# Attention row terms by a transpose and a DRAM round trip in place of TensorE transposes, with the batch's steps moved around it

## The chip, the cores and the metric

One core of one Trainium2 chip runs the whole kernel; the other cores are idle. The metric is the device time of a run in microseconds (us), and a kernel's time is the median of its runs. TensorE is called PE below, VectorE DVE, ScalarE ACT, GpSimd POOL, and the queue from which most DMAs are issued SP.

## What is computed

The input x has 64 batches of 256 rows of 256 numbers, and an adjacency matrix of 256 x 256 is shared by all batches. Each batch passes through four blocks, each with a layer norm in front and a residual sum behind. The first attention, which the change is about, has four heads:

```python
q = (norm(x) @ W).reshape(B, N, H=4, 64)
e_src, e_dst = q @ a[:64], q @ a[64:]                 # two numbers per row and head
e = e_src[:, :, None, :] + e_dst[:, None, :, :]
e = where(e >= 0, e, 0.2 * e)
attn = softmax(where(adj > 0, e, -9e15), axis=2)
x = x + elu(einsum('bijh,bjhd->bihd', attn, q))
x = x + norm(x) @ weight.T + bias
# a second attention of the same kind with one head (slope 0.01, relu)
# a mixture of 8 experts, the best 2 for each row: y = gelu(t @ w1[e]) @ w2[e]
```

The kernel never forms the sum e. The exponential of a leaky rectifier of a sum is the larger of two products, so it takes exponentials of per-row terms, and one vector instruction per half of a head gives `max(term of row i, term of row j) * mask`. For that it needs the term of row i along the free dimension, the same in all 128 partitions, while the term of row j lies in partition j already. This row of terms, spread over all partitions, is what the change makes in another way.

## The kernel before

**Steps and ranks.** The program is written in order of *steps*; three steps make a *period*, in which one batch enters and two pairs of expert blocks are worked on (phases 0, 1 and 2). Every batch and every pair is a generator. A `yield` of a positive number ends its work in this step, and the number is its rank in the next one: within a step the generators run in order of rank. A negative number leaves it in the same step, to be taken up again at that rank. Engines get their instructions in the order so made and work through them in order; an engine that waits for a semaphore holds all that is behind it. The main loop at L1138 starts batches, pairs and the scattering of results.

**A batch** (`batch_layers`, L537). In phase 2 DVE turns the batch's input into a transposed tile (L542). In phase 0 the statistics of the first norm are taken (L547; POOL raises them to the power -1/2 at L383, two norms at a time). In phase 1 `projected` (L549, matmuls at L436) makes the four heads and their terms, ACT takes the exponentials (L444), and DVE scales the heads (`scaled`, L452). In the next phase 2 and phase 0 `scores` does two heads each: PE transposes the term column, broadcast to 128 x 128, against the identity (L506), which leaves the row of terms in all partitions of a PSUM bank, and DVE forms max and mask from it (L513). In the next phase 1 `attended` multiplies (L527). Later steps do the residual, the second norm, the dense layer (L584), the second attention (`projected1`, L471; `scores1`, L495), the expert input (L635, L640), and the router (L665). ACT copies every PE transpose from PSUM to SBUF at L426.

**The pairs** (`expert_pair`, L783). A pair is 256 gathered rows of one expert. It starts in phase 1 and requests its rows there (`xr`, four DMAs at L799, and `xt`, L810), one step later its weights (`we`, L825, seven buffers). Two steps after the start DVE turns the rows (`sT`, L116), two steps on PE does the first product (L857), then the second (L872). In the last steps, when no batch is left to enter, a pair starts in every step.

**The DMA queues.** All of a period's loads and stores of these kinds are issued by SP in one order: `xr` and `xt` of the two pairs, `xblk` (the blocks that L542 turns), the two `we`, `xin` (the rows for the norm and the residual), and `out_dram<-base` (L651), which waits for ACT's L640. As the program is built, a DMA issued by SP or ACT takes one of eight semaphores in turn, in one sequence over both queues, and its issue waits until the DMA that had this semaphore eight places earlier has landed. ACT issues six DMAs in all, at the start.

Of the kernel before, what the change touches and what calls it, by code (L numbers as in the profile page):

```python
# [9 lines left out]
F32 = mybir.dt.float32  # L10
# [5 lines left out]
P = 128  # L16
# [11 lines left out]
def kernel(  # L28
# [17 lines left out]
    nc = tc.nc  # L46
    B, N, D = x.shape
    E = router.shape[0]
    H = 4
# [44 lines left out]
    def load_batch(b):  # L94
        t = io.tile([P, NT, D], F32, tag="xin", name=f"xin_{b}", bufs=6)
        nc.sync.dma_start(
            out=t, in_=x_rows[b * N : (b + 1) * N, :].rearrange("(t p) d -> p t d", p=P)
        )
        return t
# [10 lines left out]
        return t  # L110

    S = 32

    def turned(dst, blocks):

# [371 lines left out]
    def scores1(ex, me):  # L487
        pd = bank("pd", [N])
        for t in range(NT):
            nc.tensor.transpose(  # L490
                pd[:, t * P : (t + 1) * P], ex[:, t, 1:2].to_broadcast([P, P]), ident
            )
        z = work.tile([P, NT, N], F32, tag="z", name="z", bufs=6)
# [6 lines left out]
    def scores(q, heads, hs, mask, probs):  # L500

        d = D // heads
        pd = bank("pd", [len(hs), N])
        for i, h in enumerate(hs):
            for t in range(NT):
                nc.tensor.transpose(  # L506
                    pd[:, i, t * P : (t + 1) * P],
                    q[:, t, h, d + 1 : d + 2].to_broadcast([P, P]), ident,
                )
        for i, h in enumerate(hs):  # L510
            z = work.tile([P, NT, N], F32, tag="z", name="z", bufs=6)
            for j in range(NT):
                nc.vector.scalar_tensor_tensor(  # L513
                    z[:, j, :], pd[:, i, :], q[:, j, h, d + 2 : d + 3], mask[:, j, :],
                    op0=ALU.max, op1=ALU.mult,
                )
            probs.append(z)

    def attended(q, heads, probs):

        d = D // heads
        pvs = []
        for t in range(NT):
            pv = bank("pv", [heads, d + 1])
            for h, z in enumerate(probs):
                for j in range(NT):
                    nc.tensor.matmul(  # L527
                        pv[:, h, :], z[:, j, t * P : (t + 1) * P], q[:, j, h, : d + 1],
                        start=(j == 0), stop=(j == NT - 1),
                    )  # L530
# [6 lines left out]
    def batch_layers(b, c0, xng, lg):  # L537

        xb = xblk.pop(b)
        if b + BLOCKS_AHEAD < B:  # L540
            xblk[b + BLOCKS_AHEAD] = load_blocks(b + BLOCKS_AHEAD)
        xT = turned(work.tile([P, KT, N], F32, tag="xT", name="xT", bufs=4), xb)  # L542
        yield 40
        x0 = xin.pop(b)
        if b + AHEAD < B:
            xin[b + AHEAD] = load_batch(b + AHEAD)
        _, rstd = norm_stats(x0)  # L547
        yield 20
        q, pqs = projected(xT, wx0, H, rstd)  # L549
        yield -28  # L550
        scaled(q, pqs, H, rstd)
        yield 10
        probs = []
        scores(q, H, range(0, 2), masks[0], probs)
        yield 10
        scores(q, H, range(2, 4), masks[0], probs)
        yield 50
        pvs, rinv = attended(q, H, probs)
        hp = work.tile([P, NT, D], F32, tag="hp", name="hp", bufs=1)

        early = b < EARLY
# [12 lines left out]
        x1b = work.tile([P, NT, D], F32, tag="x1b", name="x1b", bufs=1)  # L574
        eng = nc.gpsimd if early else nc.vector
        eng.tensor_add(x1b, x1, bias_f[:, None, :].to_broadcast([P, NT, D]))
        yield 30
        _, rstd = norm_stats(x1)
        xT = transposed(x1)
        yield 70  # L580
        pf = bank("pf", [NT, D])
# [12 lines left out]
            )  # L594
        yield 7
        rstd = norm_squares(x2, sums)
        yield -60
        xT = transposed(x2)
        yield 20
        q, ex, me = projected1(xT, rstd, b)  # L600
        yield 25
        z = scores1(ex, me)
        yield 40
        pvs, rinv = attended(q[:, :, None, :], 1, [z])
        yield 5
        rel = work.tile([P, NT, D], F32, tag="rel", name="rel", bufs=1)
        for t, pv in enumerate(pvs):
# [9 lines left out]
            )  # L617
        yield 6
        rstd = norm_squares(x2, sums)
        yield 45  # L620

        by = small.tile([P, 2, NT], F32, tag="by", name="by")
        nc.vector.scalar_tensor_tensor(  # L623
# [159 lines left out]
    def expert_pair(j, n, ids, ef, regs, needs):  # L783

        i = j % GROUP
        upto = min(j + GROUP, n)
        if i == 0:
            _, regs["e"] = nc.values_load_multi_w_load_instructions(
                ids[0:1, 0, j:upto], engines=[mybir.EngineType.SP], min_val=0, max_val=E - 1,
                skip_runtime_bounds_check_because=WHY,  # L790
            )
            _, regs["t"] = nc.values_load_multi_w_load_instructions(
                ids[0:1, 1, j:upto], engines=[mybir.EngineType.SP], min_val=0, max_val=E * CAP,
                skip_runtime_bounds_check_because=WHY,
            )
        e_sp, t_sp = regs["e"][i], regs["t"][i]
        xr = io.tile([P, PAIR // S, KT * S], F32, tag="xr", name="xr", bufs=XBUFS)
        loads = [
            nc.sync.dma_start(  # L799
                out=xr[g * S : (g + 1) * S],  # L800
                in_=xs_d.rearrange("(t c q) f -> t q c f", c=PAIR // S, q=S)[
                    bass.ds(t_sp, 1), :, :, g * KT * S : (g + 1) * KT * S
                ].rearrange("t q c f -> (t q) c f"),
            )
            for g in range(P // S)
        ]

        xt = small.tile([P, 2, ROW - D], F32, tag="xt", name="xt", bufs=14)
        loads.append(
            nc.sync.dma_start(  # L810
                out=xt,
                in_=xs_d.rearrange("(t k p) c -> t p k c", p=P, k=2)[
                    bass.ds(t_sp, 1), :, :, D:
                ].rearrange("t p k c -> (t p) k c"),
            )
        )
        for load in loads:
            tc.add_to_no_dep_group("rows", load.ins)
# [138 lines left out]
    def begin(job, rank):  # L957
        active.append([rank, len(order), job])
        order.append(job)
# [255 lines left out]
```

## Time and profile before

| | us |
|---|---|
| median of 3 runs (lowest, highest) | 1562.9 (1556.77, 1562.9) |
| the profiled execution's own time | 1554.1 |
| its span, first to last instruction | 1552.2 |
| PE busy over the span | 1476.8 (95%) |
| DVE busy | 1210.8 (78%) |
| ACT busy | 1015.3 (65%) |
| POOL busy | 881.0 (57%) |
| q1, SP's DMA queue: share of 16 DMA engines | 36.5% |
| q0, POOL's DMA queue: share of 16 DMA engines | 23.2% |

The page is of one profiled execution. Busy time is per engine; instructions that only wait or issue a DMA are not counted. A group line gives source line, engine, operation, tiles and shapes, count, then busy time in all, mean ns of one, and the idle time just before the group with what ended it. PE's instructions are pipelined, so that "busy" and the mean of one overlap with the next; the distance between the starts of two groups is what a group costs. A line of the chain or of the waits names who waited for whom. The wait rows give total us, times and the longest. The first pairs are requested at 198 us, the last first-layer transposes run at 1279 us, and the rest of the span is expert work.

### The profile page before, as it was taken

Reading aid. Unit: us, or ns where it says so; the run is one execution under the profiler, and the core shown is the slowest. Engines: PE = TensorE matmul, PEld = TensorE weight load, DVE = VectorE, ACT = ScalarE, POOL = GpSimd, SP = SyncE. Lnnn points to the kernel's source line nnn. Section 1 sums busy time; section 2 is a strip of 40 time slices with the busy share of each in tenths; the row PEclk is TensorE's granted clock in tenths of the full one; section 3 lists DMA queues with packets and bytes.
Section 4 is the critical chain, followed back from the end, with each engine's and each line's share of the span. In section 5 each row is a group of like instructions: output and inputs, shape, how many; then the busy total and the mean of one; then the engine's idle time right before and its main releaser. Section 6 shows DMA issues by size and latency. Waiting matters only on the chain. (4 is left out here: it accounts for less than half of the span.)

```text
span 1552.2 us, 30789 instructions
## 1 busy us (share of the span) xinstructions
PE 1476.8 (95%) x8570; PEld 1308.1 (84%) x8570; DVE 1210.8 (78%) x4313; ACT 1015.3 (65%) x2387; POOL 881.0 (57%) x867
## 2 busy tenths in 40 slices
PE   6999999999999999999999999999999998879997
PEld 5888888888888888888888888888888987668885
DVE  6888888888888888888878888888788778555543
ACT  1566666767677676776767777766678888654332
POOL 2222645466657575656667575755765566644444
PEclk9999999999999999999999999999999999889999
DMA  5812233665657666566656666566586575688853
GB/s 153 224 51 69 90 101 87 158 132 131 148 127 168 134 130 141 140 137 142 138 129 153 133 159 138 127 136 143 127 178 144 111 145 115 132 200 173 156 100 51
DMA packets 361514, 207.61 MB, mean 134 GB/s; under 512 B 261496, under 2 KB 331648, under 8 KB 361344
## 3 DMA queue, kind: packets, MB, share of 16 engines
q1 hardware_dynamic: 311488, 138.31, 36.5%
q0 software_dynamic: 48864, 66.33, 23.2%
q8 instruction: 71, 1.16, 0.3%
q10 hardware_dynamic: 992, 0.99, 0.2%
q14 instruction: 99, 0.81, 0.2%
HBM read 117.43 MB, written 88.09 MB: 132 GB/s over the span
## 5 line engine op out<-in xcount | busy, mean ns | idle before, releaser
L893 POOL DMA_INDIRECT out_dram<-y,xt x258 | 410.2, 1590 | 179.8 <-issue 75.8
L527 PE MATMUL pv<-q,z 128*128 128x65 f32 (+1 forms) x2560 | 364.1, 297 | 0.0
L527 PEld LDWEIGHTS pv<-q,z 128*128 128x128 f32 x2560 | 328.0, 192 | 11.5
L872 PE MATMUL py<-w2s,hT 128*128 (+1 forms) x1224 | 284.3, 383 | 6.8 <-ACT hT L863 6.2
L965 POOL DMA_INDIRECT xs<-xng,pos x244 | 251.5, 1031 | 65.8 <-issue 58.6
L872 PEld LDWEIGHTS py<-w2s,hT 128*128 128x128 f32 x1224 | 229.7, 192 | 39.7 <-ACT hT L863 9.0
L426 ACT COPY xT<-pt 128x512 f32<-128x512 f32 x192 | 112.8, 588 | 210.8 <-PE pt L420 148.5
L857 PE MATMUL ph<-sT,we 128*128 128x256 f32 x1032 | 241.1, 384 | 0.2 <-DVE sT L116 0.2
L857 PEld LDWEIGHTS ph<-sT,we 128*128 128x128 f32 x1032 | 194.2, 193 | 25.6 <-DVE sT L116 0.7
L513 DVE SCALAR_TENSOR_TENSOR z<-pd,q,mask 128x256 f32<-128x256 f32 x512 | 210.9, 473 | 0.0
L863 ACT ACTIVATE hT<-ph,we 128x256 f32<-128x256 f32 x306 | 124.2, 471 | 63.2 <-PE ph L857 41.1
L471 PE MATMUL pq<-wx,xT 128*128 128x259 f32 x512 | 133.6, 405 | 25.3 <-ACT xT L426 19.0
L850 ACT ACTIVATE y<-y,w 128x256 f32<-128x256 f32 x258 | 112.1, 499 | 69.2 <-DVE y L882 55.5
L382 POOL TENSOR_SCALAR rstd<-mv 128x4 f32<-128x4 f32 (+1 forms) x66 | 15.7, 238 | 221.7 <-DVE by L623 203.9
L471 PEld LDWEIGHTS pq<-wx,xT 128*128 128x128 f32 x512 | 94.6, 195 | 53.0 <-ACT xT L426 28.4
L882 DVE TENSOR_TENSOR y<-py,b2s 128x512 f32<-128x512 f32 x129 | 86.3, 687 | 63.4 <-PE py L872 49.9
L401 ACT ACTIVATE off<-x,sums 128x256 f32<-128x256 f32 x256 | 129.3, 505 | 8.5 <-DVE x L591 1.1
L436 PE MATMUL pq<-wx,xT 128*128 128x268 f32 x512 | 130.2, 398 | 3.3 <-DVE xT L116 2.7
L584 PE MATMUL pf<-wfT,xT 128*128 128x256 f32 x512 | 121.3, 380 | 0.0
L635 ACT ACTIVATE xng<-x,by,rstd 128x256 f32<-128x256 f32 x128 | 70.1, 597 | 74.9 <-DVE by L623 74.8
L436 PEld LDWEIGHTS pq<-wx,xT 128*128 128x128 f32 x512 | 97.1, 194 | 21.3 <-issue 3.3
L534 DVE RECIPROCAL rinv<-pv 128x4 f32<-128x4 f32 (+1 forms) x256 | 39.0, 166 | 84.9 <-PE pv L527 65.6
(164 smaller groups left out, 2537.5 us busy)
## 6 DMA issues: line engine op xcount, KB each, us to landing
we<-wpack SPq DMA_DIRECT2D x145, 288.0 KB
xr<-xs SPq DMA_DIRECT2D x516, 64.0 KB
xblk<-in_x_dram SPq DMA_DIRECT2D x256, 64.0 KB
xin<-in_x_dram SPq DMA_DIRECT2D x64, 256.0 KB
out_dram<-base SPq DMA_DIRECT2D x61, 256.0 KB
out_dram<-y,xt POOLq DMA_INDIRECT x258
xs<-xng,pos POOLq DMA_INDIRECT x244
xs<-fill SPq DMA_DIRECT2D x9, 260.0 KB
```

Source lines behind the costliest of these rows:

```text
L401: nc.scalar.activation(off, src[:, t, :], AF.Square, bias=sums[:, t : t + 1], scale=-float(D), accum_out=sq[:, at + t : at + t + 1],)
L426: nc.scalar.copy(dst, pt)
L436: nc.tensor.matmul(pq.rearrange("p h c -> p (h c)"), xT[:, k, t * P : (t + 1) * P], wx[:, k, :], start=(k == 0), stop=(k == KT - 1),)
L471: nc.tensor.matmul(pq, xT[:, k, t * P : (t + 1) * P], wx1[:, k, :], start=(k == 0), stop=(k == KT - 1),)
L513: nc.vector.scalar_tensor_tensor(z[:, j, :], pd[:, i, :], q[:, j, h, d + 2 : d + 3], mask[:, j, :], op0=ALU.max, op1=ALU.mult,)
L527: nc.tensor.matmul(pv[:, h, :], z[:, j, t * P : (t + 1) * P], q[:, j, h, : d + 1], start=(j == 0), stop=(j == NT - 1),)
L584: nc.tensor.matmul(pf[:, t, :], xT[:, k, t * P : (t + 1) * P], wfT[:, k, :], start=(k == 0), stop=(k == KT - 1),)
L857: nc.tensor.matmul(ph[:, f, :], we[:, k * D + f * P : k * D + (f + 1) * P], xT[:, k, :], start=(k == 0), stop=(k == KT - 1),)
L863: nc.scalar.activation(hT[:, f, :], ph[:, f, :], AF.Gelu, bias=we[:, C_B1 + f : C_B1 + f + 1])
L872: nc.tensor.matmul(py[:, t, :], hT[:, f, t * P : (t + 1) * P], w2s[:, e, f * D : (f + 1) * D].rearrange("p e c -> p (e c)"), start=(f == 0 ...
L893: d = nc.gpsimd.indirect_dma_start(out=out_rows, out_offset=bass.IndirectOffsetOnAxis(ap=xt[:, t, 0:1].bitcast(I32), axis=0), in_=y[:, t, ...
L965: d = nc.gpsimd.indirect_dma_start(out=xs_d[: E * CAP * PAIR, :], out_offset=bass.IndirectOffsetOnAxis(ap=at, axis=0), in_=xe, in_offset=None,
```

## The change

- **Terms.** The eight PE transposes per batch (L506) are gone. After `scaled`, DVE transposes in 32 x 32 blocks four columns of each head of q (128 x 32 numbers) into `ut`; ACT's queue stores the rows that hold the terms to a small DRAM tile (4 KB, one per batch); a second DMA of ACT's queue reads these 4 KB back into all 128 partitions (512 KB written), straight into one half of a new tile `z4`. `scores` then reads both its tensors from SBUF and writes over that half at its end. The second attention's z has a tile of its own with one buffer.
- **Order.** The first norm is taken when the batch begins, now in phase 0, one period before its projection. The projection moves from phase 1 to phase 0, directly behind `projected1` of an earlier batch; `scaled`, the transpose and the store follow in the same step at rank 24, the spreading load at rank 52. `scores` and `attended` stay in the phases where they were, which is two and more steps later.
- **Others.** The PE transposes for L471 move ahead of the second attention's product in their step (rank 60 to 36). The `by` terms for L635 move from rank 45 to 8. The transposes for the dense layer go to rank 30, the statistics ahead of them to 21.
- **Pairs.** `we` is requested in the same step as `xr` and `xt`, one step earlier than before.

In the program as built, ACT's order in phase 0 becomes: exponentials of the second and first attention, the store (waits for DVE's `ut`), the copy for the dense layer, L635 and L640's work, the spreading load (waits for the store), the scaling of y. The 128 new DMAs take their turn in the sequence of eight semaphores. SP's order in a period becomes `xr`, `xt`, `we` of one pair, the same of the other, `xblk`, `xin`, `out_dram<-base`. In most periods the two new DMAs stand in the sequence so that two of the four `xblk` loads, or one and `xin`, wait for them. In every fourth period, for batches 22, 26 and so on to 54, it is the first `xr` of the second pair that waits for the store, and that pair's `we` that waits for the spreading load.

```diff
+    def send_terms(q, b):
+        ut = small.tile([P, S], F32, tag="ut", name="ut", bufs=1)
+        nc.vector.transpose(
+            ut.rearrange("p (t h w) -> p t h w", t=NT, h=H), q[:, :, :, HD - 1 : HD + 3]
+        )
+        ud = tc.dram_tile([S, S], F32, name=f"terms_{b}")
+        ud = ud.rearrange("c r -> (c r)").rearrange("(c p) -> c p", p=P)
+        return ut, ud
+
+    def spread_terms(ud):
+        z = work.tile([P, NT, NT, H, P], F32, tag="z4", name="z4", bufs=2)
+        nc.scalar.dma_start(
+            out=z[:, NT - 1].rearrange("p t h i -> p (t h i)"),
+            in_=rows_to_all(ud, S * S),
+        )
         return z
...
-        pd = bank("pd", [len(hs), N])
-        for i, h in enumerate(hs):
-            for t in range(NT):
-                nc.tensor.transpose(
-                    pd[:, i, t * P : (t + 1) * P],
-                    q[:, t, h, d + 1 : d + 2].to_broadcast([P, P]), ident,
-                )
...
+        for h in hs:
             for j in range(NT):
                 nc.vector.scalar_tensor_tensor(
-                    z[:, j, :], pd[:, i, :], q[:, j, h, d + 2 : d + 3], mask[:, j, :],
+                    z[:, j, :, h, :], z[:, NT - 1, :, h, :], q[:, j, h, HD + 2 : HD + 3],
+                    masks[0][:, j, :].rearrange("p (t i) -> p t i", t=NT),
                     op0=ALU.max, op1=ALU.mult,
                 )
...
+        if b:
+            x0, rstd = first_norm()
+            yield 99
+            yield 25
...
-        yield 40
-        x0 = xin.pop(b)
-        if b + AHEAD < B:
-            xin[b + AHEAD] = load_batch(b + AHEAD)
-        _, rstd = norm_stats(x0)
-        yield 20
+        if not b:
+            x0, rstd = first_norm()
+        yield 22
         q, pqs = projected(xT, wx0, H, rstd)
-        yield -28
+        yield -24
         scaled(q, pqs, H, rstd)
+        ut, ud = send_terms(q, b)
+        nc.scalar.dma_start(
+            out=ud.rearrange("c (g r) -> g c r", g=G),
+            in_=ut[2 : P : S // (NT * H), :],
+        )
+        yield -52
+        z = spread_terms(ud)
+        yield 99
         yield 10
...
-        yield 30
+        yield 21
         _, rstd = norm_stats(x1)
+        yield -30
         xT = transposed(x1)
...
-        yield -60
+        yield -36
         xT = transposed(x2)
...
-        yield 45
+        yield 8
...
-        yield 90
         we = io.tile([P, WROW], F32, tag="we", name="we", bufs=WBUFS)
         nc.sync.dma_start(
             out=we, in_=wpack[bass.ds(e_sp, 1), :, :].rearrange("e p c -> (e p) c")
         )
+        yield 90
...
-            if phase == 2 and more:
+            if more and (phase == 0 or step == 2):
...
-                    begin(nxt, 25)
+                    begin(nxt, 40 if phase == 0 else 25)
```

More of the change, by code (lines that the diff above doesn't have):

```diff
@@ L112 @@
     S = 32
+    G = P // S
     def turned(dst, blocks):
@@ L492, in scores1 @@
             )
-        z = work.tile([P, NT, N], F32, tag="z", name="z", bufs=6)
+        z = work.tile([P, NT, N], F32, tag="z1", name="z1", bufs=1)
         for j in range(NT):
@@ L497, in scores1, with scores, attended @@
             )
-        return z
-    def scores(q, heads, hs, mask, probs):
-        d = D // heads
-        pd = bank("pd", [len(hs), N])
-        for i, h in enumerate(hs):
-            for t in range(NT):
-                nc.tensor.transpose(
-                    pd[:, i, t * P : (t + 1) * P],
-                    q[:, t, h, d + 1 : d + 2].to_broadcast([P, P]), ident,
-                )
-        for i, h in enumerate(hs):
-            z = work.tile([P, NT, N], F32, tag="z", name="z", bufs=6)
+        return [z[:, j, :] for j in range(NT)]
+    def send_terms(q, b):
[12 more added lines that the diff above has]
+        )
+        return z
+    def scores(q, z, hs):
+        for h in hs:
             for j in range(NT):
                 nc.vector.scalar_tensor_tensor(
-                    z[:, j, :], pd[:, i, :], q[:, j, h, d + 2 : d + 3], mask[:, j, :],
+                    z[:, j, :, h, :], z[:, NT - 1, :, h, :], q[:, j, h, HD + 2 : HD + 3],
+                    masks[0][:, j, :].rearrange("p (t i) -> p t i", t=NT),
                     op0=ALU.max, op1=ALU.mult,
                 )
-            probs.append(z)
-    def attended(q, heads, probs):
+    def attended(q, heads, z):
         d = D // heads
@@ L524, in attended @@
             pv = bank("pv", [heads, d + 1])
-            for h, z in enumerate(probs):
+            for h in range(heads):
                 for j in range(NT):
                     nc.tensor.matmul(
-                        pv[:, h, :], z[:, j, t * P : (t + 1) * P], q[:, j, h, : d + 1],
+                        pv[:, h, :], z(j, h, t), q[:, j, h, : d + 1],
                         start=(j == 0), stop=(j == NT - 1),
@@ L537, in batch_layers, with first_norm @@
     def batch_layers(b, c0, xng, lg):
+        def first_norm():
+            x0 = xin.pop(b)
+            if b + AHEAD < B:
+                xin[b + AHEAD] = load_batch(b + AHEAD)
+            return x0, norm_stats(x0)[1]
+        if b:
+            x0, rstd = first_norm()
+            yield 99
+            yield 25
         xb = xblk.pop(b)
@@ L542, in batch_layers @@
         xT = turned(work.tile([P, KT, N], F32, tag="xT", name="xT", bufs=4), xb)
-        yield 40
-        x0 = xin.pop(b)
-        if b + AHEAD < B:
-            xin[b + AHEAD] = load_batch(b + AHEAD)
-        _, rstd = norm_stats(x0)
-        yield 20
+        if not b:
+            x0, rstd = first_norm()
+        yield 22
         q, pqs = projected(xT, wx0, H, rstd)
-        yield -28
+        yield -24
         scaled(q, pqs, H, rstd)
+        ut, ud = send_terms(q, b)
[6 more added lines that the diff above has]
+        yield 99
         yield 10
-        probs = []
-        scores(q, H, range(0, 2), masks[0], probs)
+        scores(q, z, range(0, 2))
         yield 10
-        scores(q, H, range(2, 4), masks[0], probs)
+        scores(q, z, range(2, 4))
         yield 50
-        pvs, rinv = attended(q, H, probs)
+        pvs, rinv = attended(q, H, lambda j, h, t: z[:, j, t, h, :])
         hp = work.tile([P, NT, D], F32, tag="hp", name="hp", bufs=1)
@@ L603, in batch_layers @@
         yield 40
-        pvs, rinv = attended(q[:, :, None, :], 1, [z])
+        pvs, rinv = attended(
+            q[:, :, None, :], 1, lambda j, h, t: z[j][:, t * P : (t + 1) * P]
+        )
         yield 5
```

## The prediction

> **What bounds the kernel now.** I read the busy time by stretches first, then PE's timeline over one period, the groups by shape, the waits, and SP's timeline. In the stretches, columns are length, busy time of PE, weight loads, DVE, ACT, POOL, then PE's granted clock and DMA share:
>
> ```profile
> core 0: us, PE busy (x) PEld busy (x) DVE busy (x) ACT busy (x) POOL busy (x), PEclk, DMA share, GB/s
> 350.00:1050.00 700.00, 692.36 (x4151) 619.94 (x4152) 575.52 (x1985) 498.86 (x1183) 443.27 (x423) 1.00 0.64 140
> ```
>
> While batches and pairs run together PE is busy 99%, DVE 82%, ACT 71%. PE is the bound; DVE is near enough to become it. One period on PE's timeline (start, length):
>
> ```profile
> 649.85 2.02 PE L471 MATMUL pq<-wx,xT 128*128 128x259 f32 x8 [0.24 <-issue]
> ...
> 663.39 0.60 PE L506 MATMUL pd<-ident,q 128*128 128x128 f32 x4
> 663.82 3.62 PE L857 MATMUL ph<-sT,we 128*128 128x256 f32 x16
> ...
> 668.09 1.98 PE L527 MATMUL pv<-q,z 128*128 128x257 f32 x8
> 669.91 0.60 PE L420 MATMUL pt<-ident,x 128*128 128x128 f32 x4
> 670.35 0.60 PE L506 MATMUL pd<-ident,q 128*128 128x128 f32 x4
> 671.18 1.15 PE L471 MATMUL pq<-wx,xT 128*128 128x259 f32 x4 [0.24 <-issue]
> ```
>
> From L471 to L471 it takes 21.33 us. Four transposes cost 663.82 - 663.39 = 0.43 us, though each shows 0.27. L471 comes 0.83 us after the last four, so 0.4 us is idle: only those four (0.43) cover ACT's copy of L420's result. The waits name it (us, times, longest), and show who holds SP:
>
> ```profile
> PEld pq L471 <- ACT xT L426: 28.4, 36, 3.4
> ...
> SPq L651 <- ACT base L640: 420.8, 47, 15.4
> ```
>
> The groups show the work that goes or changes side (busy us, mean ns):
>
> ```profile
> L506 PE MATMUL pd<-ident,q 128*128 128x128 f32 x512 | 77.1, 274 | 3.4 <-ACT q L444 3.4
> L513 DVE SCALAR_TENSOR_TENSOR z<-pd,q,mask 128x256 f32<-128x256 f32 x512 | 210.9, 473 | 0.0
> L614 DVE SCALAR_TENSOR_TENSOR x<-x,rel 128x256 f32<-128x256 f32 x128 | 48.7, 417 | 0.0
> ```
>
> And SP's timeline, with DVE's use of the rows it loads:
>
> ```profile
> 679.77 0.40 SPq L651 DMA_DIRECT2D out_dram<-base  x1
> 682.52 1.55 SPq L799 DMA_DIRECT2D xr<-xs  x4
> ...
> 685.22 1.86 SPq L799 DMA_DIRECT2D xr<-xs  x4
> ...
> 699.88 0.40 SPq L651 DMA_DIRECT2D out_dram<-base  x1
> ```
>
> ```profile
> 700.67 1.30 DVE L116 STREAM_TRANSPOSE sT<-xr 128x512 f32<-128x512 f32 x2
> ```
>
> SP issues a period's loads in 12 us and waits 9 for L640; rows requested by 687 are used at 700.7. An issue takes 0.4 to 0.5 us.
>
> **The Trainium skill.** "Trainium Kernel Development and Optimization", Performance Expectations, warns that matmul busy time misleads because matmuls are pipelined; the trace agrees, 0.43 for four against 0.27 each, so I price starts, not L506's 77.1 us. "Perfetto Trace Analysis", Optimizing Scalar/DVE Operations, puts DVE's access overhead at about 60 ns on SBUF and 125 on PSUM; L614 against L513, both 256 wide, differ by 56 ns. "DMA: Bandwidth & Descriptors", Anatomy of one DMA (told of POOL's path), gives some 2 us fixed, mostly the write receipt; L651's stores, from issue to the last landing in the trace, take 2.0 us in the median, so I use that. "SBUF — State Buffer", Who interferes with whom, says that a DVE instruction with two SBUF inputs contends with a POOL instruction that reads SBUF; POOL's L411 runs from 189 to 744 ns here, DVE's L614 only from 411 to 471, so POOL pays.
>
> **The change part by part.** My clock is 0 at L471's start, with the rows' own distances.
>
> *Transposes gone.* 2 x 0.43 = 0.87 us per batch on the bound, x 64 = 56 us.
>
> *L420 ahead of L527.* L527's 1.82 us (669.91 - 668.09) now covers the copy: 0.4 more, x 64 = 25 at most. A period would be 21.33 - 1.26 = 20.07. The order on PE is L471 0 to 1.85, L436 to 3.66, L420 to 4.1, L872 to 7.55, L490 and L527 to 11.3, L420 (expert input), L584 to 13.53, L857 to 17.0, L665, L420 to 18.2, L527 to 20.07.
>
> *DVE.* Eight L513 at 417 instead of 473 ns save 0.45 us; `ut` is not in the trace. It is L116's operation at a sixteenth of its 700 ns width: 0.1 to 0.7, I take 0.2. DVE stays at 17.5 us of 20.1, 87%. Behind `ut` are the norm of x, y and sT, with 0.5 to 1 us of cover before PE's L857 asks.
>
> *ACT.* Exponentials end at 4.7; `scaled` (2 x 0.4) and `ut` at 5.9. The store waits for that, about 1.2 us in which all of ACT stands: the dense copy, L635, L640, L850. It issues in 0.45; copy and L635, L640 take until 9.1, L850 until 10.8. PE asks for L635 at 11.3 and for the next copy at 11.8: 1 us of cover. When routing lengthens DVE's queue by 1 to 2.5 us (its small operations, one batch in four most), this cover is gone and L471 waits again; I charge 0.2 us a batch, 10 in all. Bounds: 0, and 0.6 a batch, 30.
>
> *Round trip.* Store issued 6.0, landed 8.1; spreading load issued about 8.3, under L640. Its 128 reads of 4 KB are four times `bias_f`'s and twice `xin`'s 256 KB, which lands in 4.0 us (median in the trace). I take 4.7, landed at 13; bounds 3.5 and 9. DVE asks at 16.6, so 3.6 us cover it; if it landed at 19, 2.4 us of DVE wait meet 2.6 us of DVE slack. Its packets, at the 0.16 us of the trace's 4,160-byte packets, take 128 x 0.16 / 16 = 1.3 us of all DMA engines a period: DMA share 0.64 to 0.70.
>
> *Norm earlier.* ACT's L444 waited 22.7 us in all for POOL's L383, mostly in the first batches; DVE and POOL do the same work. I count nothing; its xin load moves no further ahead than its buffers. `by` at rank 8 lets L635 start without its 75 us of waits: cover for the ACT sum above, no gain by itself.
>
> *SP.* In most periods `xblk` now waits for both new DMAs, so SP resumes at 13 and `out_dram<-base` goes at about 15 instead of 9; the second pair's rows are requested by 20.5 and land by 23.5, wanted at 29. No cost. `we` earlier removes no PE wait, since none on it is listed; its two issues push the second pair's rows back 0.5 us, covered. In nine batches (22 to 54 by fours) the second pair's rows wait for the store: requested 8.1 to 10.2, landed at 12.2 (2.0 to 2.8 us as now), while DVE wants them at 9.1. It stands 3 us, L591 comes 1.7 late, and L471 with it; its `we` is requested at 13, lands at 16.3, for an L857 at 15.3. I take 1.7 us a batch, 15 in all; bounds 5 and 40.
>
> *First 14 batches, without pairs.* Of a period of 14.4 us (L471 at 110.0 and 124.4) DVE is busy 85%, and routing makes some 16.3. DVE takes PE's place as the bound, and `by` waits for POOL behind L576. I give them 0.5 instead of 1.26: 10 us less. *Last batches*: new waits in SP's queue while a pair starts each step, and one `we` buffer more in use of seven: 3 us; bounds 0 and 15.
>
> *Sum.* -56 - 25 + 10 + 15 + 10 + 3 = -43, against the profiled 1554.1: 1511. The median of the runs is 8.8 above that execution, one of the three 2.7; I add half of the 8.8 and predict **1516**.
>
> **The rivals.**
> - *All covers hold:* PE stays at 20.07, the nine batches hide their wait behind the slack: -81 + 7, 1475 to 1490. For it: PE at 99% and 2.6 us of slack on DVE. Against: ACT's 1 us of cover. 0.2.
> - *Stalls take the place of the transposes:* ACT's stop at the store and DVE's queue cost 0.8 us in each of 50 batches (40 instead of 10), the nine batches 3 us each (27): -81 + 40 + 27 + 10 + 3 = -1, and with the half of 8.8, 1557 (1545 to 1571). For it: two engines above 80%. Against: the wait stands where ACT now idles 3.8 us for L420. 0.17.
> - *Slower: the spreading load lands late.* DVE's first `scores` stands in order ahead of L591's and L527's next consumers. My sum is 43 / 64 = 0.7 us a batch, the slack 2.6; from a landing at 16.6 + 2.6 + 0.7 = 19.9 on, 11.6 us after its issue instead of 4.7, the kernel is slower than before, and each further us costs 64. At 20.5: 1554 + 38 = 1592. For it: 128 partitions reading one 4 KB piece beside a DMA share of 0.64. Against: `we` (288 KB) lands in 3.3 us beside the same load. 0.13.
> - *That the transposes don't go* can be excluded: the built order has none at L506.
>
> **Numbers.** The forecast (1490 to 1545) has 0.5, the rivals 0.2, 0.17, 0.13. What a measurement of this kernel can tell from no change is 0.5%, 7.8 us: 1555 to 1571. Half of the third case lies below, so faster 0.79, same 0.08, slower 0.13. The range takes in the first rival's lower end and most of the third: 1475 to 1562; outside are 0.05 below and 0.15 above. Faster cases hold most of the chance, so it needs no second range.
>
> **What would show it.** PE: no L506, L471 to L471 at 20.1 to 20.4, and no wait of L471 for L426 beyond 10 us in all. ACT: waits for DVE's `ut` of about 1.2 us, 64 times. DVE: no wait of `scores` for the spreading load after the first batches; 3 us waits at `sT` in nine batches, and PE waits for `we` there. I am wrong if the load lands more than 8 us after its issue, if ACT waits for the store's landing as long as for `ut`, or if DVE is busy over 92% between 350 and 1050 us.

## The result, and the profile after

| us | before | after |
|---|---|---|
| median (lowest to highest, 20 runs each) | 1558.36 (1553.91 to 1564.82) | 1554.12 (1549.12 to 1560.36) |
| ratio of after to before | | 0.997 (0.9957 to 0.9983) |
| the profiled execution's own time, and its span | 1554.1, 1552.2 | 1555.0, 1553.2 |
| PE busy over the span | 1476.8 | 1433.2 |
| DVE busy over the span | 1210.8 | 1256.4 |

The change took off 4 us, where 47 were forecast (1563 to 1516). The transposes are gone from PE, so the question is where their time went. First the same views as before. While batches and pairs run together (columns as before: length, busy PE, weight loads, DVE, ACT, POOL, granted clock, DMA share):

```profile
core 0: us, PE busy (x) PEld busy (x) DVE busy (x) ACT busy (x) POOL busy (x), PEclk, DMA share, GB/s
350.00:1050.00 700.00, 689.24 (x4068) 618.14 (x4068) 617.18 (x2114) 525.24 (x1239) 465.79 (x443) 1.00 0.75 172
```

PE is still busy 98%, with fewer instructions, and DVE has risen from 82 to 88%. One period on PE's timeline:

```profile
664.21 0.64 PE L421 MATMUL pt<-ident,x 128*128 128x128 f32 x4
664.68 1.90 PE L539 MATMUL pv<-q,z 128*128 128x257 f32 x8
666.42 1.91 PE L472 MATMUL pq<-wx,xT 128*128 128x259 f32 x8
668.17 1.97 PE L437 MATMUL pq<-wx,xT 128*128 128x268 f32 x8
...
686.32 1.91 PE L472 MATMUL pq<-wx,xT 128*128 128x259 f32 x8
```

The two projections stand in a row, L539 covers ACT's copy of L421's result, and L472 to L472 takes 19.90 us. This period came out as forecast (20.1 to 20.4), even a little shorter. The groups that changed side, and the new one:

```profile
L525 DVE SCALAR_TENSOR_TENSOR z<-z,q,mask 128x256 f32<-128x256 f32 x512 | 250.5, 510 | 17.8 <-DMA z<-terms 8.7
L643 DVE SCALAR_TENSOR_TENSOR x<-x,rel 128x256 f32<-128x256 f32 x128 | 48.8, 418 | 0.0
L505 DVE STREAM_TRANSPOSE ut<-q 128x32 f32<-128x32 f32 x64 | 13.6, 212 | 2.2
```

`ut` takes 0.21 us, as forecast. But L525 takes 510 ns in the mean where L513 took 473, and where 417 was forecast. Three of the waits over the whole span (us, times, longest):

```profile
ACT xT L427 <- DVE stats L375: 130.1, 45, 7.0
...
PEld pq L472 <- ACT xT L427: 33.7, 31, 2.6
...
DVE sT L117 <- DMA xr<-xs: 17.5, 9, 2.1
```

The first is ACT's stop at the store: L427 is the next counted instruction behind it. The wait that was to go, L472 for ACT's copy, is larger in the sum than before (28.4). Between 350 and 1030 us it is 11.7, in 15 periods (before 5.3, and 10.1 more that the trace puts down to "issue"), while the kernel with the order alone (below) has none there. The third is a wait for rows that the store holds up, as forecast, nine times.

**Where it went.** DVE's copy of each batch's router products (`lg`, L698 after, L669 before) marks when a batch's layers are done. Cutting both traces, and that of one experiment told below, at the same batches gives (us):

| | before | after | order alone |
|---|---|---|---|
| to batch 0 | 81.4 | 102.0 | 86.8 |
| 0 to 13 | 203.1 | 216.0 | 193.8 |
| 13 to 17 | 84.3 | 81.9 | 82.4 |
| 17 to 49 | 686.1 | 654.7 | 668.1 |
| 49 to 63 | 335.2 | 341.3 | 329.0 |
| 63 to the end of the span | 162.1 | 157.2 | 157.2 |
| sum (the span) | 1552.2 | 1553.2 | 1517.3 |

After is 33.5 us late at batch 13, wins it back by batch 49 (-33.8), and ends level. Each column is one trace, and the first row is its least certain: five kernels whose first 17 batches are the same (order alone and four told below) have batch 0 done at 85.7 to 88.9 us, and two others, alike up to their first pairs, at 82.7 and 89.0. The start is seen on DVE's timeline of the first steps, in the kernel before:

```profile
15.34 1.65 DVE L513 SCALAR_TENSOR_TENSOR z<-pd,q,mask 128x256 f32<-128x256 f32 x4
16.91 0.70 DVE L116 STREAM_TRANSPOSE xT<-xblk 128x512 f32<-128x512 f32 x1
```

and after:

```profile
15.63 0.21 DVE L505 STREAM_TRANSPOSE ut<-q 128x32 f32<-128x32 f32 x1
...
22.03 1.92 DVE L525 SCALAR_TENSOR_TENSOR z<-z,q,mask 128x256 f32<-128x256 f32 x4 [5.14 <-DMA z<-terms]
23.87 0.70 DVE L117 STREAM_TRANSPOSE xT<-xblk 128x512 f32<-128x512 f32 x1
```

and on PE's, which waits for that L117:

```profile
24.63 3.94 PE L437 MATMUL pq<-wx,xT 128*128 128x268 f32 x8 [10.24 <-DVE xT L117]
```

The terms of batch 0 are ready at 15.8 and back at 22.0: store 1.7 us from issue to landing, spreading load 4.4. Before, DVE began its first scores at 15.34. The turning of batch 1 (L117) stands behind them in DVE's order, so PE idles 10 us, and its eight L437 then take 3.94 us, where batch 0's took 2.07: the granted clock is 0.57 from 20 to 30 us. The Trainium skill, "TensorE: Matmul & The Clock Gate", Part 1, says that the clock is low by default and that sustained activity releases it; the trace agrees, as this stretch follows those 10 us of idle time and from 30 to 40 us the granted clock is 0.94 again.

### The profile page after: what moved, and what is told of

Same layout as the page of the kernel before. It is cut to its first block, busy times and chain, and to the rows that moved or that the text cites. A ratio compares the mean times of both kernels' runs of the same rounds, so it can differ in the third digit from the quotient of the medians.

```text
span 1553.2 us, 29980 instructions
## 1 busy us (share of the span) xinstructions
PE 1433.2 (92%) x8058; PEld 1260.9 (81%) x8058; DVE 1256.4 (81%) x4377; ACT 1007.5 (65%) x2381; POOL 887.6 (57%) x869
## 5 line engine op out<-in xcount | busy, mean ns | idle before, releaser
L922 POOL DMA_INDIRECT out_dram<-y,xt x258 | 416.1, 1613 | 204.7 <-issue 57.6
L539 PE MATMUL pv<-q,z 128*128 128x65 f32 (+1 forms) x2560 | 359.1, 295 | 0.6 <-DVE z L525 0.4
L539 PEld LDWEIGHTS pv<-q,z 128*128 128x128 f32 x2560 | 327.7, 192 | 12.0 <-DVE z L525 1.0
L994 POOL DMA_INDIRECT xs<-xng,pos x244 | 256.6, 1052 | 65.7 <-issue 60.8
L525 DVE SCALAR_TENSOR_TENSOR z<-z,q,mask 128x256 f32<-128x256 f32 x512 | 250.5, 510 | 17.8 <-DMA z<-terms 8.7
L427 ACT COPY xT<-pt 128x512 f32<-128x512 f32 x192 | 112.1, 584 | 203.0 <-DVE stats L375 130.1
L437 PE MATMUL pq<-wx,xT 128*128 128x268 f32 x512 | 132.1, 402 | 33.0 <-DVE xT L117 15.7
L472 PE MATMUL pq<-wx,xT 128*128 128x259 f32 x512 | 129.5, 396 | 22.0 <-ACT xT L427 22.0
L437 PEld LDWEIGHTS pq<-wx,xT 128*128 128x128 f32 x512 | 98.0, 195 | 58.0 <-issue 15.4
L472 PEld LDWEIGHTS pq<-wx,xT 128*128 128x128 f32 x512 | 96.8, 194 | 47.8 <-ACT xT L427 33.7
L611 PE MATMUL pf<-wfT,xT 128*128 128x256 f32 x512 | 130.6, 401 | 0.0
L611 PEld LDWEIGHTS pf<-wfT,xT 128*128 128x128 f32 x512 | 99.2, 204 | 12.3
L117 DVE STREAM_TRANSPOSE sT<-xr 128x512 f32<-128x512 f32 x129 | 87.7, 699 | 18.3 <-DMA xr<-xs 17.5
```

What stands on the lines that cost most here:

```text
L427: nc.scalar.copy(dst, pt)
L437: nc.tensor.matmul(pq.rearrange("p h c -> p (h c)"), xT[:, k, t * P : (t + 1) * P], wx[:, k, :], start=(k == 0), stop=(k == KT - 1),)
L472: nc.tensor.matmul(pq, xT[:, k, t * P : (t + 1) * P], wx1[:, k, :], start=(k == 0), stop=(k == KT - 1),)
L525: nc.vector.scalar_tensor_tensor(z[:, j, :, h, :], z[:, NT - 1, :, h, :], q[:, j, h, HD + 2 : HD + 3], masks[0][:, j, :].rearrange("p (t i ...
L539: nc.tensor.matmul(pv[:, h, :], z(j, h, t), q[:, j, h, : d + 1], start=(j == 0), stop=(j == NT - 1),)
L611: nc.tensor.matmul(pf[:, t, :], xT[:, k, t * P : (t + 1) * P], wfT[:, k, :], start=(k == 0), stop=(k == KT - 1),)
```

## The experiments

My theory was that the round trip does not fit the start, that DVE's longer scores cost more where DVE is the bound, and that ACT's stop costs late. The rivals were the new order of the steps and the waits between DMAs. Each ratio is to the kernel before, timed along with it; in brackets stands its 95% interval.

**Order alone.** All batches get their terms from PE again (`pe_scores` is transposes to PSUM, then max and mask, as before), in the new order of steps:

```diff
+        by_pe = b < B
...
-        scores(q, z, range(0, 2))
+        (pe_scores if by_pe else scores)(q, z, range(0, 2))
```

> Only the order of the steps and the early request of the weights: all 64 batches get their terms by TensorE transposes. Theory A: no loss at the start (router result of batch 0 at 81 to 86 us), and the period with pairs falls only by the wait that is now covered, 0.3 to 0.4 us of 21.4: total 1540 to 1552. Theory B (the order is what costs): the start is late by 15 to 20 us here too, total 1565 to 1580.

1521.9 us, ratio 0.979 (0.976 to 0.981); the table's third column is this kernel. Theory B falls, and so does my figure: the order by itself gains 35 us in the span, and the terms over DRAM lose 36 on top of it (32 by the medians, 1554.1 less 1521.9). By stages (after less order alone), they cost 15.2 before batch 0 and 22.2 up to batch 13, gain 13.4 between 17 and 49, and cost 12.3 from 49 to 63. From 350 to 1050 us this kernel's PE has no gap:

```profile
350.00:1050.00 700.00, 700.00 (x4266) 634.11 (x4265) 591.97 (x2056) 518.76 (x1213) 450.49 (x436) 1.00 0.65 142
```

**Which part of the order.** One rank of the kernel before; then that with the early weights; then that with the other ranks, without the projections in a row and the earlier norm:

```diff
-        yield -60
+        yield -36
         xT = transposed(x2)
```

> The kernel before with one number changed: the transposes for the second projection at rank 36 instead of 60, ahead of the second attention's product. The whole order without the terms took 1521.9 us, 36 less than before. Theory: this one step makes most of it, since the product now covers ACT's copy, 0.4 to 0.6 us in each of 64 batches: 1525 to 1537. Rival: the projections in a row or the earlier norm make it: 1545 to 1557.

> The kernel before with the second projection's transposes at rank 36 and the pairs' weights requested with their rows. The rank alone took 1537.5 us, the whole order 1521.9. If the weights' request makes the rest, 1522 to 1527; if it is the projections in a row, the earlier norm and the ranks, 1535 to 1540.

> The kernel before with three of the changed ranks (second projection's transposes 36, the dense layer's 21 and 30, the expert input's terms 8), the first projection and norm where they were. Rank 36 alone took 1537.5 us, the whole order 1521.9. If the other ranks make the difference (ACT's L635 no longer waits for DVE's terms), 1522 to 1528; if it is the projections in a row and the earlier norm, 1534 to 1540.

1537.5 us (0.987, 0.983 to 0.991), 1537.7 (0.989, 0.987 to 0.990) and 1527.5 (0.981, 0.978 to 0.983). The rank alone makes 20 of the 36 us: batches 17 to 49 take 668.5 instead of 686.1, 0.55 us each, as long as in the whole order. The early weights give nothing. The other ranks give most of the rest by the medians; where, the traces don't show, as the two profiled executions have spans of 1531.5 and 1531.8. What the projections in a row add (1527.5 to 1521.9 in different sets of runs, with intervals that overlap) is not settled.

**The start and the first batches.** PE transposes in the first 3 batches, and in a second kernel in the first 17 (`b < 17`), with terms over DRAM after them:

```diff
+        by_pe = b < 3
```

> The changed kernel, but batches 0 to 2 get their row terms by TensorE transposes as before. Theory A (the loss at the start is the terms' round trip of about 6 us, which does not fit between steps of 4 us, and holds DVE, then PE, then all set-up loads): the router result of batch 0 comes at 81 to 86 us instead of 102, the total falls by 16 to 20 us, to 1534 to 1538. Theory B (the new order of the steps costs the start): it stays at 98 to 103 us and the total within 4 us of 1554. Both leave the slow vector instructions of batches 3 to 16 as they are.

> The changed kernel, but batches 0 to 16 get their terms by TensorE transposes. Theory A with the second part (in batches 1 to 16 one scores instruction of eight takes 1.37 us instead of 0.48, since with both operands in SBUF it waits for POOL's addition of 1.44 us): a further 10 to 13 us go, total 1520 to 1525, and no scores instruction of those batches is over 0.6 us. Rival: the growth of 13 us between batches 4 and 13 is the order or ACT's stop at the store, and the long instructions are hidden: total no lower than with three batches (1534 to 1538).

1544.5 us (0.992, 0.990 to 0.994): batch 0 at 90.8 us, but 0 to 13 still in 214.9. 1519.9 us (0.977, 0.974 to 0.979): batch 0 at 85.7, and 0 to 13 in 196.8 instead of 216.0. The total of the second is theory A's, and with it the loss in the first 17 batches is shown to be the terms' way over DRAM; which part of it costs what is taken up below. The first gave half of what I expected: 11 us, all of them before batch 0, where the terms cost 15. Batches 3 and on still meet short steps, and they share these with batch 0, whose way to the router takes many of them; that the rest of the 15 comes from there is argued, not tested by itself.

Is it the round trip, or that its DMAs and the experts' set-up loads hold each other through the eight semaphores? The trace shows such waits in the first 50 us. So the set-up was put off, in the changed kernel and in a control:

```diff
-            if step >= SETUP_AT and setup:
+            if setup and step >= (SETUP_AT if len(setup) > E + 1 else 24):
```

> The changed kernel with the eight experts' set-up loads begun at step 24 (some 120 us) instead of step 8, so that in the first 80 us nothing of them shares the eight semaphores or the DMA engines with the terms. Theory E (the round trip of 6 us is itself longer than the first steps, and is what holds DVE and then PE): the router result of batch 0 stays at 97 to 103 us, the total within 5 us of the changed kernel's. Theory F (terms and set-up loads wait for each other's semaphores): it comes at 87 to 93 us and the total falls by 9 to 15 us.

> Control: the kernel before with its set-up loads put off in the same way. Without the terms' DMAs neither theory expects a change: the router result of batch 0 at 79 to 83 us, the total within 4 us of before.

1554.6 us (0.998, 0.997 to 0.999), batch 0 at 99.8; control 1556.3 us (1.000, 0.998 to 1.001), batch 0 at 83.6. Theory E holds: the set-up loads have no part in it. The batches' own loads still take turns with the terms (SP's `xblk` loads wait up to 6.2 us for the store there too), but DVE waits only 0.9 us for `xblk` in the first 40 us, against 5.1 for the first spreading load.

**DVE's scores.** Three reasons for 510 instead of 417 ns were taken apart. In 14 of the batches 1 to 16, one L525 of the eight takes 1.3 to 2.1 us, mostly 1.37. POOL and DVE at such a place:

```profile
142.19 1.44 POOL L602 TENSOR_TENSOR x1b<-x,bias_f 128x512 f32<-128x512 f32 x1 [4.37 <-DVE x L599]
```

```profile
142.03 2.80 DVE L525 SCALAR_TENSOR_TENSOR z<-z,q,mask 128x256 f32<-128x256 f32 x4
```

The second of the four begins 0.51 us after the first, takes 1.37, and ends 0.3 us after POOL's addition. In the kernel before, whose scores read PSUM, four take 1.65 us:

```profile
142.04 1.65 DVE L513 SCALAR_TENSOR_TENSOR z<-pd,q,mask 128x256 f32<-128x256 f32 x4
```

The addition was moved to DVE in all batches (`EARLY = 16` to `EARLY = 0`):

> The changed kernel with the addition of the dense layer's bias on DVE in all batches, where POOL has it in the first 16. If the long scores instructions of batches 1 to 16 (1.37 instead of 0.48 us, one in eight) are held by this addition, none is over 0.6 us now; DVE saves 0.9 and spends 0.7 us a batch, so the total moves by no more than 4 us (1550 to 1556). Rival: the length has another cause (the DMAs that write into the same tile); the long ones stay, and DVE's 0.7 us a batch comes on top: 1562 to 1566.

1547.8 us (0.993, 0.990 to 0.996). From batch 1 on no scores instruction takes over 0.6 us (three of batch 0's take 0.74 to 0.86, beside other set-up work), and 6 us are gone, two more than I expected, although DVE now does the addition. 0 to 13 still takes 211.8, 18 us more than order alone (193.8). Against that, DVE has per batch 0.7 us for that addition, 0.2 for `ut` and 8 x (0.458 - 0.393) = 0.5 for scores by their starts. The two stretches, this kernel first:

```profile
99.20:311.00 211.80, 191.11 (x1154) 165.97 (x1154) 189.33 (x675) 128.82 (x352) 80.99 (x102) 0.98 0.38 112
86.80:280.60 193.80, 190.18 (x1264) 172.56 (x1262) 177.77 (x651) 130.12 (x351) 88.78 (x114) 1.00 0.33 92
```

DVE is busy 11.6 us more, 89% of a stretch that is 18 longer. The other 6.4 us are idle time on DVE, mostly waits for PE's dense product (L611): 12.0 us, against 3.9 in order alone. In the changed kernel they are 12.5, and a part of them is PE's clock: between 102 and 318 us it is granted at half in four stretches of 3.4 us, in order alone in none, and eight L611 then take 3.1 to 3.3 us instead of 1.9:

```profile
155.39 3.32 PE L611 MATMUL pf<-wfT,xT 128*128 128x256 f32 x8
```

So by this count about two thirds of what is left of the loss is DVE's own work. The rest begins with gaps on PE of up to 1.5 us just ahead of this product, in which it waits for ACT's L664 (9.1 us in all), which stands behind the store in ACT's order; how it divides between these gaps and the clock is not settled.

Then the layout, so that an instruction touches 256 neighbouring numbers:

```diff
-            ut.rearrange("p (t h w) -> p t h w", t=NT, h=H), q[:, :, :, HD - 1 : HD + 3]
+            ut.rearrange("p (h t w) -> p h t w", t=NT, h=H),
+            q[:, :, :, HD - 1 : HD + 3].rearrange("p t h w -> p h t w"),
...
-                    z[:, j, :, h, :], z[:, NT - 1, :, h, :], q[:, j, h, HD + 2 : HD + 3],
+                    z[:, j, h, :], z[:, NT - 1, h, :], q[:, j, h, HD + 2 : HD + 3],
```

> The changed kernel with the terms stored head by head, so that each scores instruction reads and writes 256 neighbouring numbers instead of two runs of 128. If the two runs cost the 65 ns by which the instruction (482 ns) is longer than the other additions from SBUF (417 ns), it falls to 415 to 425 ns and DVE's busy time by some 30 us; the total falls by 5 to 12 us, from the stretches where DVE is the bound (batches 4 to 13 and 50 to 63). If it is the overwriting in place (the second instruction waits for the first), the duration stays at 480 and the starts alternate between 0.51 and 0.40 us as now, and the total stays within 3 us of 1554.

1552.2 us (0.997, 0.996 to 0.999), mean 511 ns (median 484, after 483), starts still at 0.51 and 0.40 by turns: the layout is not it. Then the operand, at another instruction, with its factor 1.0 from SBUF:

```diff
-                x2[:, t, :], x2[:, t, :], 1.0, rel[:, t, :],
+                x2[:, t, :], x2[:, t, :], ones[:, :1], rel[:, t, :],
```

> The changed kernel with one operand given in another way: the addition of the second attention's result (417 ns in the changed kernel, scalar written in the instruction) takes its factor 1.0 from a tile in SBUF, one number per partition, as scores does. If that operand is what makes scores 480 ns, this addition takes 475 to 485 ns. If it is where the other operands lie, it stays at 415 to 420.

One run, 1554.1 us, and its group:

```profile
L643 DVE SCALAR_TENSOR_TENSOR x<-x,ones,rel 128x256 f32<-128x256 f32 x128 | 56.6, 480 | 0.0
```

418 became 480 ns. It is the scalar: L614 had its factor written in the instruction, while L513 and L525 read one number per partition. With that, 480 is about the median of L525 (483), and POOL's addition is what lifts its mean to 510. The third reason, overwriting in place, is tested with the combined kernels below.

**ACT's stop at the store.** One period of ACT in the changed kernel:

```profile
670.65 0.45 ACT L445 ACTIVATE q<-pq,rstd 128x12 f32<-128x12 f32 x2
673.19 0.52 ACTq L572 DMA_DIRECT2D terms<-ut  x1
673.76 0.59 ACT L427 COPY xT<-pt 128x512 f32<-128x512 f32 x1 [2.66 <-DVE stats L375]
```

Exponentials end at 671.1, the store goes out at 673.2: 2.1 us, which is also the median of the 64. Both new DMAs were given to SP's queue:

```diff
-        nc.scalar.dma_start(
+        nc.sync.dma_start(
             out=ud.rearrange("c (g r) -> g c r", g=G),
...
-        nc.scalar.dma_start(
+        nc.sync.dma_start(
             out=z[:, NT - 1].rearrange("p t h i -> p (t h i)"),
```

> The changed kernel with both new DMAs issued by SP's queue instead of ACT's. Theory C (ACT's stop at the store, 130 us of waits for DVE's transpose in all, is what costs in the late batches and part of the early ones): these waits vanish, batches 49 to 63 take 10 to 17 us less and the periods with pairs 0.2 us less: total 1528 to 1542. Theory D (what costs is DVE's longer queue, or that loads wait for the two new DMAs): no gain, and SP, which now waits itself for the transpose and for the store's landing, delays the loads behind: total 1550 to 1580.

1540.2 us (0.988, 0.984 to 0.991): theory C. Batches 49 to 63 take 331.9 instead of 341.3, and 17 to 49 take 645.3 instead of 654.7. The middle gain has another place than I expected. Means of the period from the batch before (batches 20 to 49, by batch number modulo 4, us):

| | 0 | 1 | 2 | 3 |
|---|---|---|---|---|
| before | 21.8 | 21.3 | 21.3 | 21.3 |
| order alone | 21.2 | 20.8 | 20.8 | 20.8 |
| after | 21.2 | 21.0 | 19.7 | 19.9 |
| after, SP's queue | 21.2 | 19.7 | 19.9 | 19.9 |

It is the one period of four in which DVE waits for the second pair's rows, up to 2.1 us, that are held by the store. SP's waits in the changed kernel show it, nine of these between 350 and 1050 us, as many as DVE's:

```profile
SPq L828 <- DMA terms<-ut: 95.5, 13, 10.9
```

With another place in the sequence of semaphores DVE's wait does not occur at all between 350 and 1050 us, and 1.3 us go. The run does not separate the two effects late. The start is no better (batch 0 at 106.9), as the round trip is no shorter. Nor is 0 to 13 (214.8): DVE waits less for the dense product there, 3.2 us, but 6.5 for the terms.

**Together.** Transposes in the first 17 and the last 14 batches; transposes in 17 and SP's queue; the same with two heads interleaved; and the same with the set-up put off:

```diff
-        for h in hs:
-            for j in range(NT):
+        for j in range(NT):
+            for h in hs:
```

> The changed kernel with TensorE transposes in batches 0 to 16 and 50 to 63, and the terms over DRAM only in the 33 batches between, where each period has two pairs and PE is the bound. Theory: over DRAM the late batches lose about 17 us against transposes (the router result of batch 49 to that of batch 63 took 345.9 us with DRAM and 329.0 with transposes), while the middle gains 12: total 1519.9 - 17 = 1503, range 1500 to 1508. Rival: what was lost late is work of pairs that is only put off, and comes back before the end: total 1516 to 1522.

> TensorE transposes for batches 0 to 16, terms over DRAM from 17 on, and their two DMAs issued by SP. If the losses are separate (start and POOL's addition, ACT's stop late, ACT's place in the sequence of semaphores in one period of four), their repairs add up: batch 17 at 363 to 366 us, batches 17 to 49 in 645, 49 to 63 in 332, total 1498 to 1504. Rival: the gains overlap, since pairs and batches share engines and what one brings forward waits for another: total no better than 1508 to 1515.

> As the kernel with transposes for 17 batches and SP's queue, but with two heads' scores interleaved, so that an instruction that overwrites its own input is not directly behind the one that reads the same. If the 0.51 us from the first start to the second is a wait of the second for the end of the first, all starts stand 0.40 us apart, DVE saves 0.4 us a batch, and the total falls by 0 to 6 us (in the one period of four in which DVE is the bound, and late). If the spacing has another cause, starts stay at 0.51 and 0.40 by turns and the total within 2 us.

> The best kernel so far (transposes for 17 batches, SP's queue, scores interleaved: 1498.4 us) with the set-up loads put off. Its first 17 batches have no terms over DRAM, so theories E and F both expect nothing at the start: total 1494 to 1502.

- Middle only: 1510.7 us (0.969, 0.965 to 0.972). Batches 49 to 63 took 332.0 instead of 346.0 (with transposes in 17 batches only), 14 of the 17; the time behind batch 63 and the time to batch 17 grew by 1 to 2 us each. Between theory and rival, 8 us short of my figure.
- With SP's queue: 1506.3 us (0.969, 0.967 to 0.970), batch 17 at 361.6, 17 to 49 in 645.0, 49 to 63 in 336.3. The repairs nearly add up; late it is 4 us more than alone.
- Interleaved: 1498.4 us (0.964, 0.962 to 0.965). Starts stand 0.40 apart, four take 1.67 us instead of 1.91. As the program is built, the instruction that overwrites its own input waits for the end of the one that reads the same, which is then one place further ahead. Up to batch 63 this gains 2.6 us, while the medians differ by 8; that size is not settled.
- Set-up put off: 1498.6 us (0.962, 0.960 to 0.964). Nothing left there, as expected.

```profile
640.18 1.67 DVE L543 SCALAR_TENSOR_TENSOR z<-z,q,mask 128x256 f32<-128x256 f32 x4
```

So the best version keeps PE's transposes in the first 17 batches, where DVE and the round trip bind, and is 56 to 58 us faster than before, 36 of which the order gives without any DMA.

## Why the prediction was wrong, point by point

By stages, my sum of -43 was: 14 first batches at -0.5, -7; 36 middle batches, 36 x -1.26 + 15 + 7 = -23; the last 14, 14 x -1.26 + 3 + 3 = -12. Measured: +33.5, -33.8 and +1.2 (with the end of the span). So the miss is 40 us in the first batches and 13 in the last, against 11 in my favour in the middle.

- *First 14 batches, "I give them 0.5 instead of 1.26".* This is the step that failed: where I still counted a gain of 7 us, the terms over DRAM cost 37 against order alone (15.2 before batch 0, 22.2 from there to batch 13). I took the later round trip's 3.6 us of cover, read from a period of 20 us, for all batches. In the first steps, of about 4 us each, there is none: DVE stood 5.1 us for the first load and 8.7 in five waits, all before 99 us. I saw that DVE becomes the bound, but in the sum the change still left it with less to do, while between batches 0 and 13 it got 15.6 us more (193.3 against 177.8 in order alone). The signs that I named did not show this: no load took over 8 us, and DVE was busy 88% in the middle, below 92.
- *DVE, "eight L513 at 417 instead of 473 ns save 0.45 us".* The sign was wrong. The row that I took, L614, differed in its scalar as well as in its memory; with the scalar from SBUF it takes 480 ns too. By starts, scores cost 0.5 us more per batch, because the instruction in place waits. The Trainium skill, "Perfetto Trace Analysis", Optimizing Scalar/DVE Operations, gives a smaller overhead on SBUF than on PSUM; with the same kind of scalar no such difference is seen here (483 ns against 473 in the median before, and interleaved starts 0.40 us apart against 0.39).
- *"So POOL pays".* DVE paid, 0.9 us in most batches from 1 to 16. The section of the Trainium skill that I cited ("SBUF — State Buffer", Who interferes with whom) also says that issue order decides who blocks, and the trace agrees: the addition began at 142.19 and the held instruction at 142.54. I had read POOL's spread of durations as a verdict. POOL's additions became longer too, from 1.27 to 1.44 us.
- *ACT, "0.2 us a batch", behind a stop of 1.2.* The stop was right in kind, but DVE reaches `ut` later, so it is 2.1 us in the median, and ACT's waits behind it are up to 7.0 late. Between 350 and 1030 us PE lost little by it (6.2 us of waits at L472 for the copy). In the last 14 batches the terms cost 12.3 us against order alone; I had charged these 3 us for SP's queue and three for ACT. That SP's queue gave 9.4 us back there fits, though it moves the semaphores too; that DVE's routing, which comes in small chunks there, is what lengthens the stop is argued.
- *Nine batches, 1.7 us each, 15.* Right in mechanism and count: nine waits of 1.8 to 2.1 us on DVE, where I expected 3; about 1.3 us of a period each, 9.4 in all measured by SP's queue.
- *Transposes, 0.87.* Right: from L472 to L472 on PE 20.8 in order alone less 19.9 to 20.0, in the periods without routing or held rows. In the period with routing only 0.3 is gained (21.17 less 20.85; the table's 21.2 for both goes by DVE's mark): PE idles 0.4 us, and DVE is busy 19.5. L420 ahead of L527, 0.4: it was 0.55 (21.33 less 20.78).
- *Round trip.* Store 1.6 and load 4.4 us in the median against 2.1 and 4.7. DVE never waited for it between 350 and 1050 us, so the slower rival did not come. The DMA share rose to 0.75, not 0.70; nothing here shows a cost of that.
- *The order, "I count nothing" beyond L420.* It gave 35 in the span, not 25, of which 9.3 fall between batches 0 and 13. This second error, which ran my way, is what kept the result level: by these sums the terms alone would have made the kernel slower.

## What to carry to other kernels

A path that adds latency must be priced in the stage with the shortest steps, at the start, not only in the steady period from which its cover was read. Before work is moved from the bound engine to its neighbour, list the stages in which the neighbour is the bound, and consider using each way only in the stages where it wins. A change with several parts should be run with the costly part left out: here the order of a few steps gave 35 us, and the part that gave the change its name, a gain only in the middle, took them away on balance.

## What the runs showed of the hardware

- A DVE instruction of 128x256 (multiply and add, fp32) took 480 ns with its scalar read from SBUF, and 418 with the scalar written in it.
- A scores instruction of DVE with both tensors in SBUF took 1.37 instead of 0.48 us beside a POOL addition that reads SBUF, and ended 0.3 us after it; with that addition on DVE none took over 0.6 us from batch 1 on.
- An instruction that waits for the end of the one directly before it, because it overwrites what that one reads, started 0.51 us after it; with one other instruction between them all starts stood 0.40 us apart.
- Spreading 4 KB of DRAM over 128 partitions (512 KB written) took 4.4 us from issue to landing in the median, 3.7 to 6.2.
